# A macaron block with slot attention on one core: order of the masked products, shape of the value state, place of its products

## The chip, the cores and the metric

The kernel runs on one core of a Trainium2 chip. A core has a matrix engine (TensorE, PE in the profile, with its weight loads under PEld), a vector engine (VectorE, DVE), a scalar engine (ScalarE, ACT), a general engine (GpSimd, POOL) and queues for transfers. They run side by side, each through its own instructions in order, and wait for one another through semaphores. Products are written to PSUM, which has eight banks of 2 KB for each of 128 partitions; everything else lies in SBUF. The metric is device time in microseconds; lower is better.

## The reference

Input x has 2 x 1024 tokens of 512 numbers in fp32. The result is x + 0.5 FFN, then + attention, then + 0.5 FFN again, each on the layer norm of its input. The FFN sends each token to one of two experts with 2048 hidden units. What the change touches is the attention, with 16 heads, keys of 64, values of 128 and 64 slots a head:

```python
z = cumlogsumexp(s, axis=2)
g = exp(concatenate([z[:, :, :1], z[:, :, :-1]], axis=2) - z)
p = exp(s - z)
def step_k(hk, x):      # for every token
    hk = hk * g_t[:, :, None, :] + k_t[..., None] * p_t[:, :, None, :]
    return hk, einsum('bhk,bhkm->bhm', q_t, hk)
pvT = softmax(okT)
def step_v(hv, x):
    hv = hv * g_t[..., None] + p_t[..., None] * v_t[:, :, None, :]
    return hv, einsum('bhm,bhmv->bhv', pv_t, hv)
```

The output of a head is then normalized over its 128 values, multiplied by a gate and projected back to 512 by Wo.

## The kernel before

The first FFN runs, then the attention, then the second FFN, whose first steps are woven into the end of the attention. The attention works on units: a batch (2), a group of four heads (4) and a tile of 128 tokens (8), 64 units in all, in that order. The decays g and p never appear: with E = exp(s) and C the running sum of E over the tokens, a tile's share of a scan is a masked product of two 128 x 128 matrices, and all earlier tiles come in through a state that is only added to. A unit's four heads are two pairs (pr); in a pair the halves j = 0 and 1 lie on partitions 0 to 63 and 64 to 127.

For a unit, in the names of the profile:
- keys and slots (kU, kV, made for two tiles at once, with the sums k on DVE), values and gates (U, V, C): projections, some by a scheme with fewer products. They fill the gaps of the unit before.
- tk: k and E transposed into kET. CT is the running sum of E (two scans on DVE), rC its reciprocal.
- Ap, masked into A: keys times queries (`scores`). ok: A with E, and the key state sk with the queries. It gives sT, is transposed to ts, and goes through the softmax (e, rs) and tu to uT.
- Bp, masked into B: slots times uT (`slot_weights`, through `masked_products` as A). svp: the tile's addition to the value state, E times v (`value_state_products`).
- ov: the outputs (`outputs`). First uT times the value state sv, for tiles that have one (c > 0), then B times v on top of it. sq is their square on ACT; ms its mean, root and reciprocal; POOL multiplies the gates sg by it; og = ov times sg on DVE.
- `update_value_state` adds svp to sv on DVE.
- to: og transposed; po: the projection by Wo; x: the sum with the rows. These come one unit later (`old` in the loop).

The value state sv is stored with zeros: for each pair, 128 partitions by 256 columns, of which a head fills one diagonal block of 64 x 128 and the other blocks stay zero from the memset (L158). So one product of 128 rows takes both heads of a pair. The update writes the two blocks with one DVE instruction each.

PSUM is full: two banks each for "pj" and "at", one each for "tr", "st", "ok" and "ov". Masked products take both "at" banks, half j = 0 in one and j = 1 in the other. "st" is used in turn by ts, the key state's products skp, the ranks rp of the last mixture, svp, and in the FFN's fast path by hC (`hidden_fast`). "ov" holds the outputs from their first product until og. A bank's next user waits until the last has been read.

The order on TensorE in the attention is written by hand: `on_pe` puts every product behind the one before it. In a loop step, `mid` is the unit whose softmax and outputs are made, `cur` the next, `old` the one before. The order around the change is: Bp of mid, svp, tk of cur, for every fourth tile the queries pq, then ov, Ap of cur, po of old. The order on DVE, ACT and POOL is laid when the program is built, from the order of the text and an estimate of when each operand is there. `issue_after` binds single steps.

Of the kernel before, what the change touches and what calls it, by code (L numbers as in the profile page):

```python
# [10 lines left out]
F32 = mybir.dt.float32  # L11
AF = mybir.ActivationFunctionType
ALU = mybir.AluOpType
AX = mybir.AxisListType

P = 128
# [7 lines left out]
H, DK, DV, M = 16, 64, 128, 64  # L24
HG = 4
NG = H // HG
NPR = HG // 2
# [22 lines left out]
def tile_macaron(  # L50
# [14 lines left out]
    nc = tc.nc  # L65
    PSUM = bass.MemoryType.PSUM

    const = ctx.enter_context(tc.tile_pool(name="const", bufs=1))
# [5 lines left out]
    ps2 = ctx.enter_context(tc.tile_pool(name="ps2", bufs=2, space=PSUM))  # L74
    ps1 = ctx.enter_context(tc.tile_pool(name="ps1", bufs=1, space=PSUM))
# [30 lines left out]
    causal = const.tile([P, NPR, P], F32, tag="causal", name="causal")  # L106
# [46 lines left out]
    nc.vector.tensor_scalar(gnh, gn, 0.5, None, ALU.mult)  # L153

    sk_st = const.tile([P, NPR, 2 * M], F32, tag="sk", name="sk")
    sv_st = const.tile([P, NPR, 2 * DV], F32, tag="sv", name="sv")
    nc.gpsimd.memset(sk_st, 0.0)
    nc.gpsimd.memset(sv_st, 0.0)  # L158


    sloti = work.tile([P, 2 * P], mybir.dt.int32, tag="e", name="sloti")
# [784 lines left out]
    def attention(att, then, then_steps, weight_steps):  # L946
# [6 lines left out]
        def on_pe(op, *args, **kw):  # L953
            with tc.issue_after(att.pe.ins) if att.pe else nullcontext():
                att.pe = op(*args, **kw)  # L955
# [143 lines left out]
        def masked_products(u, name, lT, rT):  # L1099


            m = work.tile([P, HG, P], F32, tag="msk", name=f"{name}{u.nm}", bufs=3)
            for j in range(2):
                r = slice(j * 64, (j + 1) * 64)
                pp = ps2.tile([P, NPR, P], F32, tag="at", name=f"{name}p{u.nm}_{j}")
                for pr in range(NPR):
                    on_pe(
                    nc.tensor.matmul,
                        pp[:, pr, :], lhsT=lT[r, pr, :], rhs=rT[r, pr, :],
                        start=True, stop=True,  # L1110
                    )
                nc.vector.tensor_tensor(m[:, ts(j, NPR), :], pp, causal[:, 0:NPR, :], ALU.mult)  # L1112
            return m

        def scores(u):

            u.A = masked_products(
                u, "A", u.kET[:, 0:NPR, :], u.qT[:, :, ts(u.c % 4, P)]
            )
# [77 lines left out]
        def slot_weights(u):  # L1197

            u.Bm = masked_products(u, "B", u.kET[:, NPR:, :], u.uT)

        def outputs(u):
            op = ps1.tile([P, HG, DV], F32, tag="ov", name=f"ov{u.nm}")
            for pr in range(NPR if u.c else 0):
                on_pe(
                    nc.tensor.matmul, op[:, 2 * pr : 2 * pr + 2, :].rearrange("p h v -> p (h v)"),
                    lhsT=u.uT[:, pr, :], rhs=sv_st[:, pr, :],
                    start=(pr == 0), stop=False, skip_group_check=True,
                )
            for h in range(HG):
                on_pe(  # L1210
                    nc.tensor.matmul, op[:, h, :], lhsT=u.Bm[:, h % 2 * NPR + h // 2, :],
                    rhs=u.v[:, ts(h, DV)], start=(u.c == 0), stop=True, skip_group_check=True,
                )

            sq = work.tile([P, HG, DV], F32, tag="sq", name=f"sq{u.nm}")
            nc.scalar.activation(sq, op, AF.Square)
            ms = small.tile([P, HG, 1], F32, tag="ms", name=f"ms{u.nm}")
            nc.vector.tensor_reduce(ms, sq, AX.X, ALU.add)
            nc.vector.tensor_tensor(ms, ms, u.rs, ALU.mult)
            nc.vector.tensor_tensor(ms, ms, u.rs, ALU.mult)  # L1220
            nc.scalar.activation(ms, ms, AF.Sqrt, bias=eps, scale=1.0 / DV)  # L1221
            nc.vector.reciprocal(ms, ms)
            nc.vector.tensor_tensor(ms, ms, u.rs, ALU.mult)  # L1223
            sg = u.sg.rearrange("p (h v) -> p h v", h=HG)
            u.gated = then.gated = nc.gpsimd.tensor_tensor(sg, sg, ms.to_broadcast([P, HG, DV]), ALU.mult)  # L1225
            u.og = work.tile([P, HG, DV], F32, tag="og", name=f"og{u.nm}")
            nc.vector.tensor_tensor(u.og, op, sg, ALU.mult)  # L1227

        def value_state_products(u):
            if u.c == NC - 1:  # L1230
                return
            u.svp = ps1.tile([P, NPR, DV], F32, tag="st", name=f"svp{u.nm}")
            for h in range(HG):
                j = h % 2
                on_pe(
                    nc.tensor.matmul, u.svp[j * M : (j + 1) * M, h // 2, :],
                    lhsT=u.E[:, ts(h, M)], rhs=u.v[:, ts(h, DV)], start=True, stop=True,
                )

        def update_value_state(u):  # L1240
            if u.c == NC - 1:
                return
            for j in range(2):
                r, v = slice(j * M, (j + 1) * M), ts(j, DV)
                st = sv_st[r, :, v]
                if u.c == 0:
                    nc.vector.tensor_copy(st, u.svp[r, :, :])
                else:
                    nc.vector.tensor_tensor(st, u.svp[r, :, :], st, ALU.add)

        def transpose_out(u):
            tp = ps1.tile([P, HG, P], F32, tag="tr", name=f"to{u.nm}")
# [21 lines left out]
        for b in range(B):  # L1274
            for g in range(NG):
                for c in range(NC):
                    u = Unit()
# [24 lines left out]
        for i in range(n + 2):  # L1302
            cur = units[i] if i < n else None
            mid = units[i - 1] if 1 <= i <= n else None
            old = units[i - 2] if i >= 2 else None


            def project(even, odd):
                if i >= n - 1:
                    next(then_steps)  # L1310
                for step in (odd if i % 2 else even) if cur else "":
                    if step == "v":
                        project_ahead(i)
                    else:
                        next(keys)

            if cur and i % 2 == 0:
                keys = keys_slots(cur)
            project("k", "v")
            if mid:  # L1320
                slot_scores(mid)
            project("k", "v")
            if old:
                transpose_out(old)
            if mid:
                slot_softmax(mid)
            project("kvk", "v")
            if mid:
                transpose_u(mid)
                update_key_state(mid)  # L1330
            project("vk", "v")
            with tc.issue_after(att.pe.ins):
                then.settle()
            if mid:
                slot_weights(mid)
                value_state_products(mid)
            if cur:
                transpose_keys_slots(cur)
                running_sum(cur, mid)
                queries(cur, mid)  # L1340
            project("", "")
            if cur and i % 2 == 0:
                ahead = None
            if mid:
                outputs(mid)
                update_value_state(mid)

                if mid.b == 0 and mid.c < 6 and mid.g < NG - 1:
                    with tc.issue_after(mid.gated.ins):
                        next(weight_steps)  # L1350
                        next(weight_steps)
            if cur:
                scores(cur)
            if old:
                project_out(old)
            if cur:
                if (cur.b, cur.g) == (0, NG - 1) and cur.c or (cur.b, cur.g, cur.c) == (1, 0, 0):
                    with tc.issue_after(att.pe.ins):
                        next(norm)
                if (cur.b, cur.g) == (0, NG - 1):  # L1360
                    next(norm)
                if cur.g == 0 and cur.b and cur.c in (1, 2):
                    att.load_rows(2 * cur.b + cur.c - 1)

                if cur.c >= 4 and cur.n + NC < n:
                    v = units[cur.n + NC]
                    if cur.c == 4:
                        att.load_queries(v.b, v.g)
                    elif cur.c == 5:
                        att.load_values_gates(v.b, v.g)  # L1370
                    elif cur.c == 6:
                        att.load_keys_slots(v.b, v.g)
                    else:
                        att.load_outputs(v.b, v.g)
                if cur.g == NG - 1 and cur.b == B - 1:
                    if cur.c == 1:
                        then.lead_pass()
                    elif cur.c >= 3:

                        with tc.issue_after(mid.gated.ins):  # L1380
                            next(then_steps)
# [77 lines left out]
```

## Time and profile before

| | us |
|---|---|
| time, median of 3 runs (2336.9 to 2337.27) | 2337.2 |
| the profiled execution | 2335.8 |
| its span, first to last instruction | 2334.1 |
| of it: first FFN | 524 |
| of it: attention, 64 units | 1369 |
| of it: second FFN | 441 |
| eight records of Bp, 64 rows x 128 columns | 0.72 |
| four records of ov<-sv, 128 rows x 256 columns | 1.03 |
| eight records of ov<-v,B, 128 rows x 128 columns | 1.05 |
| og on DVE, 128 x 512 | 0.69 |
| an update of half of sv on DVE, 64 x 256 | 0.42 |

A line of the profile names the engine, the line of the kernel, the operation, what it writes and reads, and the shape. Products that are recorded through `on_pe` all have its line, L955, so they are told apart by their names. An fp32 product stands as two records. TensorE's records overlap, and their ends are modelled, so the distance from start to start says what a product costs in a row of them. For a group of records in one row, the length is from the first start to the last end. An arrow in brackets names what ended an engine's idle time.

### The profile page before, as it was taken

How to read it: one execution, taken by the hardware profiler on the slowest of the kernel's cores; microseconds unless marked ns; L12 is line 12 of the kernel's file. 1: busy time of each engine (PE TensorE's matmuls, PEld its weight loads, DVE VectorE, ACT ScalarE, POOL GpSimd, SP SyncE). 2: the span in 40 equal slices, each digit the busy share in tenths (PEclk: the TensorE clock that was granted, in tenths of full speed). 3: DMA queues.
4: the chain of work that ended last, by engine and by line, in shares of the span. 5: the costliest groups of instructions: out<-in, count | busy, mean ns of one | idle time of the engine just before them, and what ended most of it. 6: DMA issues, size and time to landing. Idle time of an engine off the chain costs nothing.

```text
span 2334.1 us, 28356 instructions
## 1 busy us (share of the span) xinstructions
PE 2260.4 (97%) x10552; PEld 1560.6 (67%) x10552; DVE 1386.8 (59%) x3116; ACT 781.2 (33%) x1462; POOL 471.8 (20%) x401
## 2 busy tenths in 40 slices
PE   6999999999999999999999999999999999999998
PEld 5687787866656656666556666666665668888765
DVE  6554556556657657666666656655656776666411
ACT  2221222323334334334434333343343332222222
POOL 3523615201101101100101000000001255434000
PEclk9999999999999999999999999999999999999999
DMA  7516425231311311310401200110110303322442
GB/s 287 223 55 214 178 93 220 106 110 37 126 51 64 122 46 64 115 58 23 163 14 68 82 28 23 73 35 16 55 37 1 109 33 145 109 100 100 167 171 100
DMA packets 56938, 222.72 MB, mean 95 GB/s; under 512 B 5983, under 2 KB 13151, under 8 KB 38880
## 3 DMA queue, kind: packets, MB, share of 16 engines
q1 hardware_dynamic: 51232, 203.52, 24.5%
q0 software_dynamic: 5280, 16.85, 1.8%
q8 instruction: 84, 1.38, 0.2%
q10 hardware_dynamic: 288, 0.52, 0.1%
q14 instruction: 54, 0.44, 0.1%
HBM read 189.86 MB, written 31.54 MB: 95 GB/s over the span
## 4 chain that ended last, share of the span: by engine, by line
PE 80%; DVE 10%; issue 5%; DMA 2%; ACT 1%; POOL 1%; SPq 0%; POOLq 0%; another core or an unknown queue 0%; DVEq 0%; ACTq 0%
PE U L955 9%; PE po L955 8%; PE oa L679 6%; PE hU L612 6%; PE V L955 5%; PE pq L955 5%; PE o L679 5%; PE kU L955 4%; PE kV L955 4%; PE ov L955 4%; PE hV L612 3%; PE hp L515 3%; PE op L734 3%; PE C L955 3%; PE ok L955 2%
## 5 line engine op out<-in xcount | busy, mean ns | idle before, releaser
L1225 POOL TENSOR_TENSOR sg<-sg,ms 128x512 f32<-128x512 f32 x64 | 67.7, 1058 | 1190.5 <-DVE ms L1223 1171.9
L955 PE MATMUL po<-wo,oT 128*128 128x512 f32 x512 | 236.6, 605 | 0.0
L515 PE MATMUL hp<-xsT,wfc 128*128 128x256 f32 (+1 forms) x768 | 148.9, 348 | 11.3 <-DMA wfc<-in_w_fc_dram 6.4
L955 PEld LDWEIGHTS po<-wo,oT 128*128 128x128 f32 x512 | 92.0, 189 | 99.5 <-issue 91.8
L515 PEld LDWEIGHTS hp<-xsT,wfc 128*128 128x128 f32 x768 | 127.2, 192 | 34.5 <-issue 14.4
L734 PE MATMUL op<-wp,a 128*128 128x512 f32 x320 | 143.2, 593 | 0.0
L1221 ACT ACT_TABLE_LOAD x64 | 82.1, 1283 | 161.1 <-DVE ms L1220 155.3
L502 DVE SCALAR_TENSOR_TENSOR t<-hp,r 128x256 f32<-128x256 f32 (+1 forms) x96 | 36.3, 378 | 153.7 <-ACT r L501 148.7
L955 PE MATMUL U<-vgT,X 128*128 128x512 f32 x256 | 120.7, 594 | 0.0
L955 PE MATMUL pq<-xnT,wq 128*128 128x512 f32 x256 | 112.5, 592 | 0.0
L1130 DVE RECIPROCAL rC<-CT 128x256 f32<-128x256 f32 x64 | 111.4, 1740 | 0.6
L612 PE MATMUL hU<-xsT,wfc 128*128 128x256 f32 x384 | 100.4, 383 | 1.0 <-ACT e L619 1.0
L734 PEld LDWEIGHTS op<-wp,a 128*128 128x128 f32 x320 | 59.7, 190 | 60.9 <-issue 57.4
L1112 DVE TENSOR_TENSOR A<-Ap,causal 128x256 f32<-128x256 f32 x128 | 53.1, 420 | 54.6 <-PE Ap L955 53.1
L501 ACT ACTIVATE r<-hp 128x256 f32<-128x256 f32 (+1 forms) x96 | 33.2, 347 | 154.5 <-PE hp L515 148.8
L955 PEld LDWEIGHTS pq<-xnT,wq 128*128 128x128 f32 x256 | 47.4, 190 | 53.6 <-issue 53.6
L612 PEld LDWEIGHTS hU<-xsT,wfc 128*128 128x128 f32 x384 | 72.4, 191 | 14.4 <-issue 2.9
L955 PEld LDWEIGHTS U<-vgT,X 128*128 128x128 f32 x256 | 49.1, 192 | 48.2 <-issue 46.5
L1163 ACT ACT_TABLE_LOAD x63 | 80.8, 1283 | 1.1
L1001 ACT ACTIVATE th<-sg 128x512 f32<-128x512 f32 x64 | 40.4, 631 | 112.1 <-DVE sg L999 106.8
L1227 DVE TENSOR_TENSOR og<-ov,sg 128x512 f32<-128x512 f32 x64 | 44.2, 690 | 55.3 <-POOL sg L1225 55.3
L1256 ACT ACTIVATE oT<-to,gnh 128x512 f32<-128x512 f32 x64 | 44.0, 687 | 86.8 <-PE to L955 79.6
(296 smaller groups left out, 5075.2 us busy)
## 6 DMA issues: line engine op xcount, KB each, us to landing
wfc<-in_w_fc_dram SPq DMA_DIRECT2D x48, 1024.0 KB
wp<-in_w_proj_dram SPq DMA_DIRECT2D x48, 1024.0 KB
vgT<-vgs SPq DMA_DIRECT2D x16, 1024.0 KB
wv<-in_w_v_dram SPq DMA_DIRECT2D x8, 1024.0 KB
ksT<-kss SPq DMA_DIRECT2D x8, 1024.0 KB
wo<-in_w_o_dram SPq DMA_DIRECT2D x8, 1024.0 KB
xs<-xs SPq DMA_DIRECT2D x6, 1032.0 KB
wks<-in_w_ks_dram SPq DMA_DIRECT2D x24, 256.0 KB
```

Of the source, the lines that this page charges most:

```text
L515: m.mark = nc.tensor.matmul(hp, lhsT=wfc[:, dc * HQ + hc * P : dc * HQ + (hc + 1) * P], rhs=xT[:, dc, :], start=(dc == 0), stop=(dc == DC ...
L612: m.mark = nc.tensor.matmul(bank, lhsT=left[:, d, :], rhs=right[:, d, :], start=start and d == 0, stop=d == 1, skip_group_check=True,)
L679: nc.tensor.matmul(bank[:, t, :], lhsT=left(q)[:, ts(t, P)], rhs=right(q), start=first and q == 0 and (t == 0 or last), stop=last and q == ...
L734: nc.tensor.matmul(ops[j], lhsT=a[hc][:, ts(j, P)], rhs=wp[:, ts(hc, D)], start=(ck == 0 and hc == 0), stop=(ck == NHQ - 1 and hc == HQ // ...
L955: att.pe = op(*args, **kw)
L1112: nc.vector.tensor_tensor(m[:, ts(j, NPR), :], pp, causal[:, 0:NPR, :], ALU.mult)
L1130: nc.vector.reciprocal(u.rC, u.CT)
L1163: nc.scalar.activation(u.u, u.u, AF.Exp)
L1221: nc.scalar.activation(ms, ms, AF.Sqrt, bias=eps, scale=1.0 / DV)
L1225: u.gated = then.gated = nc.gpsimd.tensor_tensor(sg, sg, ms.to_broadcast([P, HG, DV]), ALU.mult)
L1227: nc.vector.tensor_tensor(u.og, op, sg, ALU.mult)
L1256: nc.scalar.activation(u.oT, tp, AF.Copy, scale=gnh)
```

## The change

Four edits. The masked products are issued pair by pair, with the halves j in turn, both banks being taken ahead; the two multiplications by the mask follow. The value state loses its zeros: 128 partitions by 128 columns for each pair, half j in partitions 64 j to 64 j + 63; the memset goes, and the update is one DVE instruction over all partitions. The state's part of the outputs is four products of 64 rows by 128 columns instead of two of 128 by 256, with the halves in turn, and it moves from `outputs` to a new function that is called right behind the masked B and ahead of svp. The outputs of the halves lie in two banks: those of j = 0 in "ov", those of j = 1 in one half of "st", whose other half is svp. So Square and the product by the gates become two instructions each, and the flags that start an accumulation are set for the first product in a bank alone.

```diff
--- before.py
+++ after.py
@@ -153,9 +153,8 @@
     nc.vector.tensor_scalar(gnh, gn, 0.5, None, ALU.mult)
 
     sk_st = const.tile([P, NPR, 2 * M], F32, tag="sk", name="sk")
-    sv_st = const.tile([P, NPR, 2 * DV], F32, tag="sv", name="sv")
+    sv_st = const.tile([P, NPR, DV], F32, tag="sv", name="sv")
     nc.gpsimd.memset(sk_st, 0.0)
-    nc.gpsimd.memset(sv_st, 0.0)
 
 
     sloti = work.tile([P, 2 * P], mybir.dt.int32, tag="e", name="sloti")
@@ -1100,16 +1099,19 @@
 
 
             m = work.tile([P, HG, P], F32, tag="msk", name=f"{name}{u.nm}", bufs=3)
-            for j in range(2):
-                r = slice(j * 64, (j + 1) * 64)
-                pp = ps2.tile([P, NPR, P], F32, tag="at", name=f"{name}p{u.nm}_{j}")
-                for pr in range(NPR):
+            pp = [
+                ps2.tile([P, NPR, P], F32, tag="at", name=f"{name}p{u.nm}_{j}") for j in range(2)
+            ]
+            for pr in range(NPR):
+                for j in range(2):
+                    r = slice(j * 64, (j + 1) * 64)
                     on_pe(
-                    nc.tensor.matmul,
-                        pp[:, pr, :], lhsT=lT[r, pr, :], rhs=rT[r, pr, :],
+                        nc.tensor.matmul,
+                        pp[j][:, pr, :], lhsT=lT[r, pr, :], rhs=rT[r, pr, :],
                         start=True, stop=True,
                     )
-                nc.vector.tensor_tensor(m[:, ts(j, NPR), :], pp, causal[:, 0:NPR, :], ALU.mult)
+            for j in range(2):
+                nc.vector.tensor_tensor(m[:, ts(j, NPR), :], pp[j], causal[:, 0:NPR, :], ALU.mult)
             return m
 
         def scores(u):
@@ -1198,22 +1200,35 @@
 
             u.Bm = masked_products(u, "B", u.kET[:, NPR:, :], u.uT)
 
+
+
+        def state_outputs(u):
+            st = ps1.tile([P, 2, NPR, DV], F32, tag="st", name=f"svp{u.nm}")
+            u.svp = st[:, 1]
+            u.op = ps1.tile([P, NPR, DV], F32, tag="ov", name=f"ov{u.nm}"), st[:, 0]
+
+            for pr in range(NPR if u.c else 0):
+                for j in range(2):
+                    r = slice(j * M, (j + 1) * M)
+                    on_pe(
+                        nc.tensor.matmul, u.op[j][:, pr, :], lhsT=u.uT[r, pr, :],
+                        rhs=sv_st[r, pr, :], start=(pr == 0), stop=False, skip_group_check=True,
+                    )
+
         def outputs(u):
-            op = ps1.tile([P, HG, DV], F32, tag="ov", name=f"ov{u.nm}")
-            for pr in range(NPR if u.c else 0):
-                on_pe(
-                    nc.tensor.matmul, op[:, 2 * pr : 2 * pr + 2, :].rearrange("p h v -> p (h v)"),
-                    lhsT=u.uT[:, pr, :], rhs=sv_st[:, pr, :],
-                    start=(pr == 0), stop=False, skip_group_check=True,
-                )
+            def heads(t, j):
+                return t.rearrange("p (r j) v -> p j r v", j=2)[:, j]
+
             for h in range(HG):
                 on_pe(
-                    nc.tensor.matmul, op[:, h, :], lhsT=u.Bm[:, h % 2 * NPR + h // 2, :],
+                    nc.tensor.matmul, u.op[h % 2][:, h // 2, :],
+                    lhsT=u.Bm[:, h % 2 * NPR + h // 2, :],
                     rhs=u.v[:, ts(h, DV)], start=(u.c == 0), stop=True, skip_group_check=True,
                 )
 
             sq = work.tile([P, HG, DV], F32, tag="sq", name=f"sq{u.nm}")
-            nc.scalar.activation(sq, op, AF.Square)
+            for j in range(2):
+                nc.scalar.activation(heads(sq, j), u.op[j], AF.Square)
             ms = small.tile([P, HG, 1], F32, tag="ms", name=f"ms{u.nm}")
             nc.vector.tensor_reduce(ms, sq, AX.X, ALU.add)
             nc.vector.tensor_tensor(ms, ms, u.rs, ALU.mult)
@@ -1224,29 +1239,27 @@
             sg = u.sg.rearrange("p (h v) -> p h v", h=HG)
             u.gated = then.gated = nc.gpsimd.tensor_tensor(sg, sg, ms.to_broadcast([P, HG, DV]), ALU.mult)
             u.og = work.tile([P, HG, DV], F32, tag="og", name=f"og{u.nm}")
-            nc.vector.tensor_tensor(u.og, op, sg, ALU.mult)
+            for j in range(2):
+                nc.vector.tensor_tensor(heads(u.og, j), u.op[j], heads(sg, j), ALU.mult)
 
         def value_state_products(u):
             if u.c == NC - 1:
                 return
-            u.svp = ps1.tile([P, NPR, DV], F32, tag="st", name=f"svp{u.nm}")
             for h in range(HG):
                 j = h % 2
                 on_pe(
                     nc.tensor.matmul, u.svp[j * M : (j + 1) * M, h // 2, :],
-                    lhsT=u.E[:, ts(h, M)], rhs=u.v[:, ts(h, DV)], start=True, stop=True,
+                    lhsT=u.E[:, ts(h, M)], rhs=u.v[:, ts(h, DV)], start=(u.c == 0), stop=True,
+                    skip_group_check=True,
                 )
 
         def update_value_state(u):
             if u.c == NC - 1:
                 return
-            for j in range(2):
-                r, v = slice(j * M, (j + 1) * M), ts(j, DV)
-                st = sv_st[r, :, v]
-                if u.c == 0:
-                    nc.vector.tensor_copy(st, u.svp[r, :, :])
-                else:
-                    nc.vector.tensor_tensor(st, u.svp[r, :, :], st, ALU.add)
+            if u.c == 0:
+                nc.vector.tensor_copy(sv_st, u.svp)
+            else:
+                nc.vector.tensor_tensor(sv_st, u.svp, sv_st, ALU.add)
 
         def transpose_out(u):
             tp = ps1.tile([P, HG, P], F32, tag="tr", name=f"to{u.nm}")
@@ -1333,6 +1346,7 @@
                 then.settle()
             if mid:
                 slot_weights(mid)
+                state_outputs(mid)
                 value_state_products(mid)
             if cur:
                 transpose_keys_slots(cur)
```

## The prediction

> **What bounds the kernel now.** First the page's engine line and its chain of work that ended last; then the busy time of the attention stage, where every line of the change runs; then one unit of that stage in order of time; then what TensorE waited for there.
>
> ```profile
> PE 2260.4 (97%) x10552; PEld 1560.6 (67%) x10552; DVE 1386.8 (59%) x3116; ACT 781.2 (33%) x1462; POOL 471.8 (20%) x401
> PE 80%; DVE 10%; issue 5%; DMA 2%; ACT 1%; POOL 1%; SPq 0%; POOLq 0%; another core or an unknown queue 0%; DVEq 0%; ACTq 0%
> ...
> 524.00:1893.00 1369.00, 1350.95 (x6565) 839.92 (x6564) 874.71 (x2082) 536.49 (x888) 152.38 (x135) 1.00 0.17 60
> ```
>
> The third line is the attention stage: length, then busy time (count) of PE, weight loads, DVE, ACT, POOL; granted clock 1.00. TensorE is busy 1351 of 1369 us, DVE 875. A microsecond taken off TensorE here is a microsecond off the end, as long as nothing that TensorE waits for becomes late. The stage is 64 units of 21.4 us. This is one (batch 1, first head group, third token tile); columns are start, length, engine, line, operation, tile, shape, count, idle before.
>
> ```profile
> 1258.04 0.72 PE L955 MATMUL Bp<-uT,kET 64*128 64x128 f32 x8
> 1258.69 0.66 PE L955 MATMUL svp<-v,E 128*64 128x128 f32 x8
> 1258.83 0.75 DVE L1112 TENSOR_TENSOR B<-Bp,causal 128x256 f32<-128x256 f32 x2
> ...
> 1259.66 0.27 PE L955 MATMUL tk<-ident,E 128*128 128x128 f32 x1
> 1259.77 1.03 PE L955 MATMUL ov<-sv,uT 128*128 128x256 f32 x4
> 1260.59 0.86 DVE L1125 TENSOR_TENSOR_SCAN CT<-ones,CT,kET 128x128 f32<-128x128 f32 x2 [0.29 <-ACT kET L1097]
> 1260.64 1.05 PE L955 MATMUL ov<-v,B 128*128 128x128 f32 x8
> 1261.37 0.39 DVE L1249 TENSOR_TENSOR sv<-svp,sv 64x256 f32<-64x256 f32 x1
> 1261.68 1.74 DVE L1130 RECIPROCAL rC<-CT 128x256 f32<-128x256 f32 x1
> 1261.73 0.60 ACT L1216 ACTIVATE sq<-ov 128x512 f32<-128x512 f32 x1 [1.17 <-PE ov L955]
> 1262.28 3.70 PE L955 MATMUL po<-wo,oT 128*128 128x512 f32 x8
> 1263.35 0.62 DVE L1218 TENSOR_REDUCE ms<-sq 128x4 f32<-128x512 f32 x1
> 1264.00 0.43 DVE L1249 TENSOR_TENSOR sv<-svp,sv 64x256 f32<-64x256 f32 x1
> ...
> 1266.01 0.69 DVE L1269 TENSOR_TENSOR x<-po,x 128x512 f32<-128x512 f32 x1 [0.54 <-PE po L955]
> ...
> 1268.44 0.69 DVE L1227 TENSOR_TENSOR og<-ov,sg 128x512 f32<-128x512 f32 x1 [1.22 <-POOL sg L1225]
> ...
> 1269.05 0.41 DVE L1058 TENSOR_TENSOR k<-kV,kp 128x256 f32<-128x256 f32 x1
> ...
> 1269.82 1.03 PE L955 MATMUL kV<-ksT,X 128*128 128x256 f32 x4
> 1270.68 0.60 PE L955 MATMUL to<-ident,og 128*128 128x128 f32 x4
> ```
>
> TensorE has no gap from Bp to po. Behind it DVE runs CT, a state update, rC, ms, with no gap after CT; it rests 0.54 us before x and 1.22 us before og. One fp32 product is two records. In the waits of the stage TensorE waits for og 3.6 us in 4 places, for DVE's k 3.2 us in 6, for x 1.1 us in 3. In the tail there is one more:
>
> ```profile
> PE hC L612 <- DVE sv L1249: 1.3, 1, 1.3
> ```
>
> **Part 1, the alternation of the masked products.** Bp's 8 records take 0.72 us. The last alone lasts 0.272, so the eight starts lie within 0.45 us, 64 ns apart. The full-array ov<-v,B takes 1.05, the last 0.275: 111 ns apart. So the 64-row products of the two halves already run side by side, two every 112 ns (single records: the halves start 14 ns apart), though the program gives all of one half first. Here the Trainium skill (TensorEngine Tiling (Array Packing), When to Use Tiling) says that a contraction of 64 rows or less allows two row tiles and up to 2x. Taken as a gain still to be had, it would halve 128 products of 8 x 0.111 = 0.89 us: 57 us. The row says that it has been taken. I go by the row: **0**. The bound above: if the new order broke the overlap, +0.44 us x 128 = +56 us. The ok<-A,E products alternate between column halves today and their 8 records start within 0.39 us, so I give that little.
>
> **Part 2, the state's share of the outputs.** Removed, in the 56 units that have a state (64 less the 8 first tiles): ov<-sv, 4 records of 256 columns, from 1259.77 to 1260.64, 0.87 us (4 x 216 ns). Added behind Bp: 4 products of 64 rows x 128 columns, 8 records. No row shows them; the nearest is Bp, the same shape, just before them. At its pace of 112 ns a pair: 4 x 112 = 0.45 us. Side by side they cost 0.45, one after the other 0.89; I take 0.45, since the two halves write different banks (ov and st) as Bp's do. Net -0.42 us x 56 = **-23.3 us**. The same skill page (Key Properties) says that a change of tiling mode drains the array. The trace has the price: ov<-v,B to the 64-row products takes 205 ns where 112 would do, 93 ns more. By that rule a separate place for these products would cost two switches, 0.19 us of the 0.42. They stand in the same run as Bp, svp follows as before, so the number of switches stays: no charge.
>
> **Part 3, what comes closer together.** ov<-v,B now follows the tk transposes directly. It needs the masked B, done at 1259.58; it would start 0.42 earlier after Bp, at about 1260.2. Covered by 0.6 us. (First tiles already do so, with 0.20 us spare.) The new products need the st bank, so the key state's adds must be over; those end 0.4 to 1.0 us before Bp starts in nearly all units. Covered.
>
> Relative to tk, everything from ov<-v,B on is 0.87 us earlier on TensorE. DVE's row CT, rC, ms hangs on tk and doesn't move with it. It loses one update: two ops of 64x256 (0.39 and 0.43) become one of 128x256 (the masks of that size take 0.42). So the DVE chain comes about 0.4 earlier. Then og in two pieces: two 128x256 masks take 0.75 together, og 0.69, +0.06. Square in two pieces: +0.1 at most, covered since ms starts 1.0 us after sq ends. So DVE gains 0.38 where TensorE gains 0.87; what hands over from DVE to TensorE loses 0.49 us of slack.
> - to<-og: og ends 1269.13, to starts 1270.68, 1.55 spare. Covered. The units with 0.06 to 0.15 spare now (first, the sixth tile of the fourth group, and two in the tail): together **+0.8**.
> - x: 0.54 of idle covers it, just.
> - k: ends 1269.46, kV<-ksT,X starts 1269.82, 0.36 spare, so a new wait of 0.13. This happens in even tiles only; listing the spare time of the 17 such units with a state that don't wait now gives 0 to 0.27 each, **+2.0**. Seven more (two under the layer norm, five with token sums ahead of x or already late) wait now and pay 0.44 each: **+3.1**. Below that: DVE's order is laid when the program is built, and k is ready before og; put first, as in first tiles today, it costs nothing.
>
> A rule that speaks against the change: the skill (PSUM — Partial Sum Buffer, PSUM bank collisions raise a hardware error) says that two engines may not touch one bank and quadrant in the same cycle. The update of sv now reads the bank st, into which ov<-v,B writes and from which Square and og read. Held apart, sv waits for the last ov<-v,B and Square's second half, about 1.0 us after the last ov record starts. By its row sv runs 0.05 us before that record, and 0.87 later after the change: a wait of some 0.2 us for rC and og behind it, from a slack of 1.06 that is left at to. It hits only k: another 0.2 x 24 = 5 us if sv keeps its place; put between ms and its next step, where the second update is now, nothing. I take 0 and keep 5 for the range.
>
> **Part 4, the st bank held longer.** It is free only after og, not after the sv update. The next user in a unit is ts, which stands behind to, and to needs og anyway: 0. But the last mixture's hC uses st. The line above has it at 1861.5, right after the sv update; og of that unit ends at 1874.1. And hC at 1883.7, where the last tile had no st, would wait for og at 1893.0. Other products can fill in; between 0 and 12 us. I take **+3**.
>
> The memset removed (0.51 us, POOL at 3.6 us) is hidden: the first product waits until 17.3 us.
>
> **Sum:** -23.3 + 0.8 + 2.0 + 3.1 + 3 = -14.4 us. The profiled execution took 2335.8 us with a span of 2334.1; the three runs have a median of 2337.2. I take the difference off the median: 2337.2 - 14.4, about **2323**.
>
> **The rivals.** (a) *Nearly all arrives*: DVE's order is laid with k first, the tail fills, -20 to -24: 2315. For it: 1.2 us idle ahead of og in which k fits. (b) *Half is given back*: sv stalled by the bank (+5) and a tail of 6 to 8 us: 2331. For it: the rule above; against it: the slack at to. (c) *Slower*: the state's products don't run in pairs, since they lie in two accumulation banks and wait for one another or for st. Eight records at 111 ns cost 0.89, as much as was removed; the 8.9 us of waits remain: 2346. It decides from where the eight take over 0.7 us (23.3 - 8.9 = 14.4 us over 56 units is 0.26, on top of 0.45). Against it: Bp's pairs use two banks as well. (d) *No change*: nothing of the overlap is bound by TensorE; against it, 1351 of 1369 us.
>
> **How the numbers follow.** The main forecast (2317 to 2328) 0.50, (a) 0.20, (b) 0.15, (c) 0.10, (d) or a balance of these 0.05. Faster by over 0.2% (4.7 us, about what a measurement tells from no change): all of main and (a), most of (b): 0.82. Within: 0.07. Slower: 0.11. The range takes in (a) and the middle of (b): 2311 to 2333.
>
> **What would show it.** Masked products still 0.72 us for 8; the eight new records ending about 0.45 us after Bp's; no ov<-sv of 256 columns; tk followed by ov<-v,B at 109 ns; one sv of 0.42 per unit; more waits of kV for k and x, some 5 us; hC behind og in the tail. Wrong it would be if the new records start 112 ns apart singly, or if to, ts or ov<-v,B wait in every unit.

## The result, and the profile after

The changed kernel takes 2324.8 us, the median of five runs (2319.8 to 2326.2), where the kernel before took 2337.1 beside it (2334.2 to 2337.3). The ratio is **0.9948 [0.9933, 0.9962]**: half a per cent faster. Its profiled execution took 2324.6 us with a span of 2322.8, against 2335.8 and 2334.1. The prediction was 2323.

The page's engine line and its chain of work that ended last come first, then the busy times of the attention stage (length, then PE, weight loads, DVE, ACT, POOL):

```profile
PE 2244.2 (97%) x10776; PEld 1542.2 (66%) x10776; DVE 1355.5 (58%) x3124; ACT 783.6 (34%) x1526; POOL 470.5 (20%) x400
PE 67%; issue 12%; DVE 12%; POOL 3%; ACT 2%; DMA 2%; SPq 0%; POOLq 0%; DVEq 0%; ACTq 0%
...
524.00:1880.00 1356.00, 1332.05 (x6788) 820.53 (x6789) 846.60 (x2090) 538.31 (x952) 153.48 (x137) 1.00 0.18 61
```

PE lost 18.9 us of busy time in the stage (1350.95 to 1332.05), but the stage became only 13 shorter, as its idle time grew from 18.0 to 24.0. TensorE is still the bound, but its share of the chain fell from 80 to 67%; DVE's rose from 10 to 12%, and "issue", time in which an engine waited for nothing that the profile shows, from 5 to 12%.

The same unit as shown of before, now at 1245.92, in order of time. TensorE first, from Bp to the outputs:

```profile
1245.92 0.71 PE L954 MATMUL Bp<-uT,kET 64*128 64x128 f32 x8
1246.47 0.27 PE L954 MATMUL ov<-sv,uT 64*128 64x128 f32 x1
1246.48 0.27 PE L954 MATMUL svp<-sv,uT 64*128 64x128 f32 x1
1246.58 0.27 PE L954 MATMUL ov<-sv,uT 64*128 64x128 f32 x1
...
1246.80 0.27 PE L954 MATMUL ov<-sv,uT 64*128 64x128 f32 x1
1246.81 0.27 PE L954 MATMUL svp<-sv,uT 64*128 64x128 f32 x1
1247.01 0.66 PE L954 MATMUL svp<-v,E 128*64 128x128 f32 x8
...
1247.98 0.27 PE L954 MATMUL tk<-ident,E 128*128 128x128 f32 x1
1248.09 0.39 PE L954 MATMUL ov<-v,B 128*128 128x128 f32 x2
```

The eight new records start in pairs, 7 ns apart within a pair and some 110 ns from pair to pair, and take 0.45 us where the two products of 256 columns took 0.87. From Bp's first record to svp<-v,E it is 1.09 us in 45 of 48 units and 1.15 or 1.16 in the other three, where it is 0.64 in the tiles without a state. (Those for the second half bear the name svp, since they write the other half of that bank.) The masks stay at 0.71. From the last tk to ov<-v,B it is 109 ns.

The end of the same unit, from the reciprocal rC to the transposes of og:

```profile
1249.81 1.75 DVE L1132 RECIPROCAL rC<-CT 128x256 f32<-128x256 f32 x1
1251.47 0.63 DVE L1233 TENSOR_REDUCE ms<-sq 128x4 f32<-128x512 f32 x1
1253.46 0.69 DVE L1282 TENSOR_TENSOR x<-po,x 128x512 f32<-128x512 f32 x1 [0.56 <-PE po L954]
1256.20 0.42 DVE L1243 TENSOR_TENSOR og<-ov,sg 128x256 f32<-128x256 f32 x1 [1.22 <-POOL sg L1240]
1256.54 0.41 DVE L1243 TENSOR_TENSOR og<-svp,sg 128x256 f32<-128x256 f32 x1
1256.87 0.41 DVE L1262 TENSOR_TENSOR sv<-svp,sv 128x256 f32<-128x256 f32 x1
1257.20 0.41 DVE L1057 TENSOR_TENSOR k<-kV,kp 128x256 f32<-128x256 f32 x1
1257.67 1.13 PE L954 MATMUL kV<-ksT,X 128*128 128x256 f32 x4 [0.24 <-DVE k L1057]
```

This is what the prediction did not have. In the same unit of the kernel before, one update of sv stood between CT and rC and the other behind ms; og was followed by k at once. Now the one update stands behind both pieces of og, straight ahead of k, and TensorE waits for k: 0.24 us of idle time, and the kV products, whose weights come late too, take 1.13 in place of 1.03. Counted from the first tk, og starts 0.56 us earlier than before (8.60 for 9.16), but k only 0.17 (9.60 for 9.77). What TensorE waited for in the stage (us in total, places, longest):

```profile
PE kV L954 <- DVE k L1057: 8.2, 23, 0.9
PE kV L954 <- DVE x L1282: 2.8, 1, 2.8
PE to L954 <- DVE og L1243: 2.5, 4, 1.1
```

The kernel before had this line there:

```profile
PE kV L955 <- DVE k L1058: 3.2, 6, 0.8
```

**Where the 11.3 us of the span lie.** The starts of Bp in the two traces give the gain of each unit. Units are counted from 0, and so are the eight tiles of a head group: even tiles are the first, third, fifth and seventh. A period goes from one unit's Bp to the next unit's, and is named by the unit that it leads into. The period that holds a state's run is 0.43 us shorter when nothing is late: 56 x 0.43 = 24.1 us. It arrives in nearly every period in front of an even tile. In the periods in front of an odd tile, where the even tile's wait for k falls, the step is 0.01 to 0.13 in most (and up to +0.65 in front of the second tile, behind a first tile that has no state's run). Over the periods into units 1 to 22 and 32 to 61, 52 periods with 45 such runs (19.4 us), only 7.9 arrived; the 26 even tiles there gave 11.2 back. The periods into units 24 to 31, under the layer norm, gained 8.6 where the runs give 3.0. The first unit started 1.5 earlier. One period, into unit 23, lost 2.25: DVE's order has a layer-norm statistic ahead of CT that waits for a DMA there, x comes late, and kV waits 2.8 us for it (the second line). The tail, from unit 61 to the end of the attention, took 2.7 (some 4.0 if the gains of its three runs are counted in), the second feed-forward part another 1.7.

### The profile page after: what moved, and what is told of

Its sections match the earlier page's. It is cut to its first block, busy times and chain, and to the rows that moved or that the text cites. A ratio compares the mean times of both kernels' runs of the same rounds, so it can differ in the third digit from the quotient of the medians.

```text
span 2322.8 us, 28879 instructions
## 1 busy us (share of the span) xinstructions
PE 2244.2 (97%) x10776; PEld 1542.2 (66%) x10776; DVE 1355.5 (58%) x3124; ACT 783.6 (34%) x1526; POOL 470.5 (20%) x400
## 4 chain that ended last, share of the span: by engine, by line
PE 67%; issue 12%; DVE 12%; POOL 3%; ACT 2%; DMA 2%; SPq 0%; POOLq 0%; DVEq 0%; ACTq 0%
PE U L954 8%; PE oa L678 6%; PE hU L611 6%; PE po L954 5%; PE o L678 4%; PE pq L954 4%; PE V L954 4%; PE hp L514 3%; PE op L733 3%; PE hV L611 3%; PE kV L954 3%; PE kU L954 2%; PE C L954 2%; DVE rC L1132 2%; PE svp L954 2%
## 5 line engine op out<-in xcount | busy, mean ns | idle before, releaser
L1233 DVE TENSOR_REDUCE ms<-sq 128x4 f32<-128x512 f32 x64 | 41.2, 644 | 78.2 <-ACT sq L1231 78.2
L1127 DVE TENSOR_TENSOR_SCAN CT<-ones,CT,kET 128x128 f32<-128x128 f32 x112 | 48.1, 471 | 51.5 <-ACT kET L1096 51.5
```

What stands on the lines that cost most here:

```text
L1127: nc.vector.tensor_tensor_scan(u.CT[:, pr, :], ones, u.kET[:, NPR + pr, :], prev.CT[:, pr, P - 1 : P] if u.c else 0.0, ALU.mult, ALU.add,)
```

## The experiments

The kernel before ran at 2337.1, 2335.7 and 2332.9 us on the chips of these runs, so kernels are compared by their ratio to it. Each diff is against the changed kernel where nothing else is said.

**1. The alternation of the masks alone** (label alt_only), in the kernel before:

```diff
-            for j in range(2):
-                pp = ps2.tile([P, NPR, P], F32, tag="at", name=f"{name}p{u.nm}_{j}")
-                for pr in range(NPR):
...
+            pp = [
+                ps2.tile([P, NPR, P], F32, tag="at", name=f"{name}p{u.nm}_{j}") for j in range(2)
+            ]
+            for pr in range(NPR):
+                for j in range(2):
```

> The kernel before with the alternation of the masked products alone. My theory: the halves ran side by side already, so the eight records of Bp stay at 0.71 to 0.72 us and the time stays at 2337 within 2 us. Rival (the alternation brings the gain): some 12 us less, 2325.

Measured: 2332.8 us, ratio 0.9985 [0.9976, 0.9994], span 2333.4. Its timeline shows the same unit's mask:

```profile
1256.74 0.71 PE L955 MATMUL Bp<-uT,kET 64*128 64x128 f32 x8
```

0.72 has become 0.71: the halves of a pair start 7 ns apart in place of 14, and the pairs at the same pace. Nearly every unit's period is 0.01 us shorter, some 1 us in all; the remaining 2 or so of the 3.5 us by the ratio are single steps elsewhere (2.2 us into unit 30, 1.5 into unit 59), and 1.7 lost again at unit 63. In front of unit 30 DVE's order differs in two small instructions ahead of the masks, and the wait for og there is 0.5 us shorter; in the period into unit 59 DVE's order is the same as before, and the cause was not traced. For the masks the alternation is worth next to nothing.

**2. The whole change without any alternation** (no_alt), both in the masks and in the state's products:

```diff
-            for pr in range(NPR):
-                for j in range(2):
+            for j in range(2):
+                for pr in range(NPR):
...
-            for pr in range(NPR if u.c else 0):
-                for j in range(2):
+            for j in range(2):
+                for pr in range(NPR if u.c else 0):
```

> The changed kernel with the halves not alternating any more, neither in the masked products nor in the state's products: all of half 0, then all of half 1. My theory: TensorE still pairs them, the eight state records take 0.45 us, the time stays at 2325 within 2 us. Rival (pairs need the alternation): the state's records take 0.89 us and the masked products 0.89, so 0.44 x 56 + 0.44 x 128, up to 80 us more.

Measured: 2330.2 us, ratio 0.9974 [0.9963, 0.9986]: some 6 us slower than the change. Neither the 2325 of the theory nor the loss of all overlap by the rival. TensorE at the state's run:

```profile
1250.91 0.72 PE L954 MATMUL Bp<-uT,kET 64*128 64x128 f32 x8
1251.46 0.27 PE L954 MATMUL ov<-sv,uT 64*128 64x128 f32 x1
1251.47 0.37 PE L954 MATMUL svp<-sv,uT 64*128 64x128 f32 x1
1251.57 0.27 PE L954 MATMUL ov<-sv,uT 64*128 64x128 f32 x1
1251.68 0.27 PE L954 MATMUL svp<-sv,uT 64*128 64x128 f32 x1
...
1251.90 0.27 PE L954 MATMUL svp<-sv,uT 64*128 64x128 f32 x1
1252.10 0.33 PE L954 MATMUL svp<-v,E 128*64 128x128 f32 x2
```

The masks still overlap in full, and the first record of the second half (1251.47) starts ahead of the first half's second (1251.57), although it is issued behind all of them. But in the run that follows the masks the second half's second record starts 0.21 us behind its first (1251.47 to 1251.68) where 0.11 is the pace. From there that half is one slot late: from the first new record to svp<-v,E it is 0.64 us (1251.46 to 1252.10) where the change has 0.54 (1246.47 to 1247.01). In the unit starts it is 0.10 or 0.11 us in 45 of the periods with a state's run; 56 of these are 5.9 us. The ratios give about 6, with an uncertainty of some 4, and the two profiled executions differ by 3.5, as single periods went the other way (0.8 each into units 37, 45 and 53). So the alternation does next to nothing for the masks, and in the run that continues them it is worth, by the count of the steps, about 6 us, half of what the change gained.

**3. The update of sv ahead of og** (sv_first), to test what stands in k's way:

```diff
             u.gated = then.gated = nc.gpsimd.tensor_tensor(sg, sg, ms.to_broadcast([P, HG, DV]), ALU.mult)
+            update_value_state(u)
             u.og = work.tile([P, HG, DV], F32, tag="og", name=f"og{u.nm}")
...
                 outputs(mid)
-                update_value_state(mid)
```

> The changed kernel with the update of the value state moved ahead of og in the text, so that DVE runs it in the gap behind ms and not between og and k. My theory (the update of 0.41 us behind og makes k late and kV waits): each of the 32 even tiles gets 0.33 us back, 10 us, to 2315. Rival (the wait comes from TensorE being 0.87 us earlier, and og is late by itself): og moves later by as much and 2325 stays. A second rival: the update waits for Square on the shared bank and holds up the chain to og, slower than 2325.

Measured: 2316.2 us, ratio 0.991 [0.9895, 0.9925], span 2316.9. In its timeline, the same unit:

```profile
1251.12 0.41 DVE L1263 TENSOR_TENSOR sv<-svp,sv 128x256 f32<-128x256 f32 x1
...
1255.63 0.41 DVE L1244 TENSOR_TENSOR og<-svp,sg 128x256 f32<-128x256 f32 x1
1255.96 0.41 DVE L1057 TENSOR_TENSOR k<-kV,kp 128x256 f32<-128x256 f32 x1
1256.43 1.13 PE L954 MATMUL kV<-ksT,X 128*128 128x256 f32 x4
```

The update is back behind ms, k follows og, and the wait is down to this line:

```profile
PE kV L954 <- DVE k L1057: 1.9, 6, 0.5
```

Outside units 22 to 32 nearly every even tile is 0.33 us shorter, the time from the start of one such DVE update to the next. So that one instruction's place costs 0.33 us in each of 23 tiles. A remnant stays: the kV products still take 1.13 us.

**4. og behind k, in the changed kernel** (k_first). The two pieces of og go into a function that is called in the next step of the loop, ahead of the transposes that read them, with the update of sv behind it:

```diff
+            def gate_outputs():
+                u.og = work.tile([P, HG, DV], F32, tag="og", name=f"og{u.nm}")
+                for j in range(2):
+                    nc.vector.tensor_tensor(heads(u.og, j), u.op[j], heads(sg, j), ALU.mult)
...
             if old:
+                old.gate_outputs()
+                update_value_state(old)
                 transpose_out(old)
...
                 outputs(mid)
-                update_value_state(mid)
```

> The changed kernel with og and the update of the value state written behind k, so that DVE runs k first. My theory (k behind og and the update is the whole of the wait of kV): the wait of kV for k is gone, 0.43 us in 24 even tiles and some 0.5 in the 8 first tiles, 14 us, to 2311. Rival (another hand-over is next, to waiting for og, which comes 0.33 us later): no more than half of it, 2318 or above.

Measured: 2308.3 us, ratio 0.988 [0.9865, 0.9895], span 2306.9. The stage, and then the same unit in its timeline:

```profile
524.00:1866.00 1342.00, 1328.38 (x6792) 823.71 (x6793) 849.96 (x2091) 539.15 (x953) 154.16 (x138) 1.00 0.18 62
```

```profile
1253.79 0.42 DVE L1245 TENSOR_TENSOR og<-ov,sg 128x256 f32<-128x256 f32 x1 [1.22 <-POOL sg L1240]
1254.13 0.41 DVE L1057 TENSOR_TENSOR k<-kV,kp 128x256 f32<-128x256 f32 x1
1254.46 0.41 DVE L1245 TENSOR_TENSOR og<-svp,sg 128x256 f32<-128x256 f32 x1
1254.86 1.03 PE L954 MATMUL kV<-ksT,X 128*128 128x256 f32 x4
1255.12 0.41 DVE L1266 TENSOR_TENSOR sv<-svp,sv 128x256 f32<-128x256 f32 x1
```

k lies between the pieces of og here, sv behind them, and kV is back at 1.03 us with no idle time ahead of it. The waits view has no line of kV for k left, and from the fifth unit on the even tiles outside units 22 to 32 are 0.41 to 0.67 us shorter, with a few of 1.1. That is what they had given back. The stage's idle time fell from 24.0 to 13.6 us. Another 5.1 us came at one place, the period into unit 59, which the next run explains in part.

**5. The same in the kernel before** (before_k_first): is deferring og a gain by itself, whatever the change did? The diff is that of run 4 with the one og of that kernel, its two updates of sv left in place, and an order to issue og after k:

```diff
             if old:
+                with tc.issue_after(att.k1.ins):
+                    old.gate_outputs()
                 transpose_out(old)
```

> The kernel before, with og held behind k on DVE in the even tiles. There kV waited for k in 6 places, 3.2 us in all. My theory (the wait of kV is mostly made by the change, which brings TensorE 0.87 us nearer): 3 us less than the kernel before, about 2333. Rival (k first is worth the same with or without the change): some 15 us less, 2320.

Measured: 2325.5 us, ratio 0.9969 [0.9958, 0.9981], span 2323.5: 7 us gained, between the two expectations. kV's waits for k are gone, in steps of 0.38 (three times), 0.6 (twice) and 1.1, together 3.4 us, near the 3 of the theory. The rest is 5.2 us at unit 59, 2.3 at unit 30, and 2.5 lost at unit 63. Unit 59 is where the work ahead of the feed-forward part begins; the 5 us there come with a deferred og in either kernel and are no wait for k. In the kernel before, four waits for that work's rows (xn and xsT), 3.0 us in all, stand in this period, and they are gone. So of the 16 us that run 4 gains over the change, about 5 belong to unit 59 and some 1.7 to units 33 and 61, and these would come without the change; most of the rest undoes the waits that the change made.

**6. Is it og or sv that must go behind k?** (sv_k_first): as run 4, but with the update of sv left behind `outputs`. The diff is against run 4:

```diff
             if old:
                 old.gate_outputs()
-                update_value_state(old)
                 transpose_out(old)
...
                 outputs(mid)
+                update_value_state(mid)
```

> The changed kernel with k ahead of og, and the update of the value state ahead of both, in the gap behind ms. My theory: with k first nothing that TensorE waits for is behind the update, so its place is worth nothing more, within 2 us of 2308. Rival (the chain to og is next): with the update ahead of it og is later, and to waits, 2312 or more.

Measured: 2308.5 us, ratio 0.9895 [0.988, 0.991], span 2305.2. Its timeline, the same unit:

```profile
1246.83 0.63 DVE L1233 TENSOR_REDUCE ms<-sq 128x4 f32<-128x512 f32 x1
1247.37 0.41 DVE L1266 TENSOR_TENSOR sv<-svp,sv 128x256 f32<-128x256 f32 x1
```

Unit by unit it runs as k_first does (no step differs by over 0.02 us in units 2 to 22 and 31 to 61). Once og isn't ahead of it in the program's text, the update runs behind ms again, in the same bank, and no longer lies in k's way.

**7. The state's products in a run of their own** (separate): moved from behind Bp into `outputs`, straight ahead of ov<-v,B, so that two changes of the tiling mode (the split of the array that a row names, 64*128 or 128*128) are added.

```diff
         def outputs(u):
             def heads(t, j):
                 return t.rearrange("p (r j) v -> p j r v", j=2)[:, j]

+            for pr in range(NPR if u.c else 0):
+                for j in range(2):
...
-                    lhsT=u.E[:, ts(h, M)], rhs=u.v[:, ts(h, DV)], start=(u.c == 0), stop=True,
+                    lhsT=u.E[:, ts(h, M)], rhs=u.v[:, ts(h, DV)], start=True, stop=True,
```

> The changed kernel with the state's products moved back to their old place, right ahead of ov<-v,B, in a run of their own. My theory: two more changes of tiling mode, 0.19 us x 56 = 10.4 us more TensorE work; but TensorE comes 0.64 us later to kV, so the wait for k goes in the 24 even tiles that have a state, 0.43 us x 24 = 10.3 back: 2325, the same. Rival 1 (the wait is not one of distance): 2335. Rival 2 (a change of mode costs nothing here): 2314.

Measured: 2340.6 us, ratio 1.0035 [1.0022, 1.0047], span 2339.0. By the ratios that is some 20 us over the change, and slower than the kernel before. TensorE there:

```profile
1261.24 0.27 PE L954 MATMUL tk<-ident,E 128*128 128x128 f32 x1
1261.44 0.37 PE L954 MATMUL ov<-sv,uT 64*128 64x128 f32 x1
1261.45 0.37 PE L954 MATMUL svp<-sv,uT 64*128 64x128 f32 x1
1261.66 0.27 PE L954 MATMUL ov<-sv,uT 64*128 64x128 f32 x1
...
1261.89 0.27 PE L954 MATMUL svp<-sv,uT 64*128 64x128 f32 x1
1262.09 0.49 PE L954 MATMUL ov<-v,B 128*128 128x128 f32 x2
1262.41 0.39 PE L954 MATMUL svp<-v,B 128*128 128x128 f32 x2
```

The edge into the 64-row mode takes about 203 ns where 109 would do, and so does the first step behind it (1261.44 to 1261.66, 0.21 against 0.11). The way back has the same two: 0.20 from the last svp<-sv to ov<-v,B, and the first two records of ov<-v,B take 0.49 where later pairs take 0.39. Together 0.39 us for the way in and out; nearly every period with a state's run in front of an even tile is 0.39 or 0.40 us longer than in the change. In the rest it is 0.2 to 0.3 in most: the waits for k became fewer there, and new ones for x take part of their place:

```profile
PE kV L954 <- DVE k L1057: 7.0, 11, 1.3
PE kV L954 <- DVE x L1283: 5.0, 16, 0.6
```

56 x 0.39 = 21.8 us is the price of the place. The 63 periods together are 20.3 us longer than in the change: less than the price in front of odd tiles, more than it under the layer norm (1.2 to 3.2 us in each of four periods), where the waits were not followed up.

**8. The tail** (tail_bank): k_first, with the second half of the outputs of the last unit but one in the bank "ok" instead of "st", so that hC of the feed-forward part need not wait for og there.

```diff
-            u.op = ps1.tile([P, NPR, DV], F32, tag="ov", name=f"ov{u.nm}"), st[:, 0]
+            second = st[:, 0]
+            if u.n == len(units) - 2:
+                second = ps1.tile([P, NPR, DV], F32, tag="ok", name=f"ow{u.nm}")
+            u.op = ps1.tile([P, NPR, DV], F32, tag="ov", name=f"ov{u.nm}"), second
...
-                    lhsT=u.E[:, ts(h, M)], rhs=u.v[:, ts(h, DV)], start=(u.c == 0), stop=True,
+                    lhsT=u.E[:, ts(h, M)], rhs=u.v[:, ts(h, DV)], start=(u.c == 0 or u.n == len(units) - 2), stop=True,
```

> k_first, and in addition the second half of the outputs of the last unit but one lies in the bank ok, not in st, so that st is free for hC right after the update of the value state. My theory (hC waits for og on the shared bank in the tail and this costs about 2 us): 2306. Rival (other products fill in for hC): 2308, the same.

Measured: 2305.8 us, ratio 0.9881 [0.9866, 0.9896], span 2304.9. By the times it can't be told from k_first. The traces show the step: first k_first, then this kernel.

```profile
1840.74 0.41 DVE L1245 TENSOR_TENSOR og<-svp,sg 128x256 f32<-128x256 f32 x1
1841.07 0.41 DVE L1266 TENSOR_TENSOR sv<-svp,sv 128x256 f32<-128x256 f32 x1
1841.70 1.03 PE L611 MATMUL hC<-xsT,wfc 128*128 128x256 f32 x4
```

```profile
1824.53 0.42 DVE L1269 TENSOR_TENSOR sv<-svp,sv 128x256 f32<-128x256 f32 x1 [0.29 <-PE svp L954]
...
1826.97 1.13 PE L611 MATMUL hC<-xsT,wfc 128*128 128x256 f32 x4
...
1843.84 0.41 DVE L1248 TENSOR_TENSOR og<-ow,sg 128x256 f32<-128x256 f32 x1
```

Counted from the start of its unit hC comes 13.2 us earlier, 2 us behind the update, and the period into unit 63 is 1.8 us shorter. What this is worth isn't shown: the rest of the kernel takes 1.3 us longer, and sv_k_first, with hC behind og, has a period into unit 63 that is 1.6 shorter than k_first's as well.

The update itself runs 19 us ahead of og, although it stands behind og in the text in this kernel as well. In this unit alone the two read different banks. The kernel before fits this: its update stands behind og in the text too, they read different banks, and it runs ahead of og. In sv_first and sv_k_first the update stands ahead of og in the text, shares the bank with it, and runs ahead of it. So the update is held behind og where both hold, the shared bank and the later place in the text; either alone does not do it.

The best kernels are k_first, sv_k_first and tail_bank, 1.05 to 1.2% under the kernel before and 0.5 to 0.7% under the change by the ratios.

## Why the prediction was right, and where it was not

- **Part 1, 0.** Right. The rows of before showed pairs already, and 7 ns for each pair's second start is nearly all that the order changed (run 1). The rule of two row tiles, taken as a gain to be had, would have been 57 us out.
- **Part 2, -23.3.** Right: 0.43 us in each of 56 periods, 24.1, seen where nothing else was late. The new records run in pairs as Bp's do. What was not seen is that this pace depends on the order in which the program gives them (run 2): for about 6 us of it the alternation is needed.
- **The charge for a separate place.** The trace of before gave 93 ns for an edge, and the prediction doubled it to 0.19 us. The next record behind each edge is late by another 0.1, so the way in and out costs 0.39 (run 7). The rows of before had this too: Bp's second pair starts 213 ns behind its first, the others at 112, and the prediction's mean of 64 ns between starts hides the long step. The Trainium skill (TensorEngine Tiling (Array Packing), Key Properties) says that the change drains the array; nearly all of Part 2's gain would have gone into it, not half. Since the change makes no such switch, the sum was not touched.
- **Part 3, k: +2.0 and +3.1.** This is the term that was mis-sized. The even tiles gave back 11.2 us in the 52 undisturbed periods alone. The step that failed is the one that takes the DVE chain's "about 0.4 earlier" for k as well. It holds for og (0.56 us in the unit shown). But of two updates ahead of og one went away and the other moved to the one place, between og and k, where it costs time, so that k is only 0.17 earlier. Instead of the new wait of 0.13, most even tiles with a state lost 0.44 to 0.56. Five first tiles, where k stood ahead of og before and stands behind og and sv now, lost 0.45 to 0.65 each, which the sum had at nothing. The working of the bank rule named a place for the update, "put between ms and its next step, where the second update is now, nothing", and took that. It did not come about, since st holds what og and sv both read and sv stands behind og in the text (runs 3, 6 and 8). The 0.33 us are shown by run 3, and the rest of the wait by run 4.
- **The stall on a shared bank**, one engine held up by another's use of it, is in no row: in the unit shown sv runs over 7 us behind Square's second half, so that the case did not arise. The 0 taken was right, the reason for looking at that bank another one.
- **to and x.** to waits for og 2.5 us where it was 3.6, so +0.8 was not due; x, but for unit 23, stayed covered, as said.
- **Part 4, +3.** Right in the order of events: hC comes behind og in both places. The tail took 2.7 us, 4.0 with the gains of its own runs counted in, which is near the 3; how much of it is hC's wait stays open (run 8).
- **What the sum did not have**: units 24 to 31, 5.6 us more than their runs give. Behind three tiles there (26, 28 and 30) DVE's order in the changed kernel has k ahead of og where the kernel before had og first, and 2.3 us of waits are gone. Another 2.6 came at unit 30, where the alternation alone brings 2.2 (run 1), and 0.7 at unit 25. This balances the mis-sized k, 11.2 us for 5.1, and the sum had no reason to expect it. So 2323 was hit by two errors of about equal size, which is luck, and its nearness to 2324.8 says less than the points above. The 1.7 us in the second feed-forward part and the 1.5 gained ahead of the first unit were not traced; the first unit alone starts between 533.0 and 537.8 us in the runs above.

Of the rivals, (c) fell with the pairs, and (d) with the half per cent gained. (a)'s mechanism, k first, is the right one to want but did not happen by itself; run 4 had to write it, and got more than (a) gave. (b) had it right that about half is given back, though its 2331 was too high, and the way was another than its stall.

## What to carry to other kernels

In this kernel two results in one bank of the accumulator tied their readers to the order of the text. Before putting a long-lived half beside a short-lived one, list which instructions of the slower engine will now stand behind which, and who waits for them; writing the urgent one first in the text was enough here (runs 3, 4 and 6). In a sum of gains, an instruction that "goes away" from an engine must be placed as well as counted: 0.41 us of DVE work cost nothing behind ms and 0.33 us per tile ahead of k. And put products of a small tiling mode where that mode is already running, in turn between the halves.

## What was not expected of the hardware

- **A change of the tiling mode is paid twice**: 93 ns at the edge and about 100 more on the next record, in each direction, 0.39 us for the round trip (run 7). The second charge is not the mode's alone: the kV products that waited for k, with no change of mode ahead of them, have it as well (0.32 us from their first to their second start where 0.22 is the pace), and so each of those waits cost 0.1 us more than its idle time.
- **The order of issue counted in the continued run, and hardly in the masks.** Given one half first, the masks overlap fully (14 ns within a pair against 7), but the eight records that follow them in the same mode lose one slot of about 0.1 us (run 2). In the masks the second record of both halves is late by 0.1 in either order. The masks stand directly behind a change of mode and the state's products do not; that this is the reason was not tried.
